# Second layer of an adaptive feed-forward network: the last four blocks in 256-token strips, gates after the fold product, and another order of the low-rank chunks

## The chip, the cores and the metric

The kernel runs on one core of a Trainium2 chip, in float32. Its time is the device time in microseconds of that core; a median of several runs is compared. The engines are TensorE (PE, with its weight loads as PEld), VectorE (DVE), ScalarE (ACT), GpSimd (POOL) and SyncE (SP), which only issues transfers here.[...]

## The reference, cut to what matters

There are 32 x 128 tokens of width 128. Layer 0 (`x = x + L0_ffn(L0_cond(...))`) is left as it is by the change. Layer 1 is this:

```python
def _L1_cond_ref(x, t_emb, W_router, router_bias, s_w1, s_w3, s_w2, r_w1, r_w2):
    for e in range(N_SHARED):                                    # 2 shared experts, width 256
        h = jax.nn.silu(x_flat @ s_w1[e].T) * (x_flat @ s_w3[e].T)
        shared_out = shared_out + h @ s_w2[e].T
    shared_out = shared_out / N_SHARED
    s = jax.nn.sigmoid((router_in @ W_router.T).astype(jnp.float32))
    ...                                                          # the two best of 8 -> gates_full
    for e in range(N_EXPERTS):                                   # 8 routed experts, width 128
        h = jax.nn.gelu(x_flat @ r_w1[e].T, approximate=False)
        routed_out = routed_out + h @ r_w2[e].T * gates_full[:, e:e + 1]
    return (shared_out + routed_out) / (N_SHARED + TOP_K)

def _L1_ffn_ref(x, U1, V1, b1, U2, V2, b2):                      # rank 32, width 512
    P = jnp.einsum('bsd,dr->bsr', x, U1)
    H = jax.nn.gelu(jnp.einsum('bsr,rf->bsf', P, V1) + b1)
    Q = jnp.einsum('bsf,fr->bsr', H, U2)
    return jnp.einsum('bsr,rd->bsd', Q, V2) + b2

x = x + _L1_ffn_ref(_L1_cond_ref(x, cond, ...), U1, V1, b1, U2, V2, b2)
```

## The kernel before, in words

The tokens lie transposed (128 features on the partitions) in eight blocks of 512 tokens, `xall`; four blocks are a set, `sb` 0 and 1. Layer 0 ends at 800 us of the profile. Its feed-forward part is 64 units of 9.89 us, and its last fold products still lie between the first two units of layer 1.

Nothing of layer 1's middle has the full width: the down weights of its experts are multiplied once with `U1` (`fold`, `fold_down`, L249), so that each expert gives 32 rows per token at once. `into` (L848) puts the 32 rows of four blocks side by side on the four quarters of the 128 partitions, one column tile of TensorE for each block, and adds all experts of a set in one PSUM bank, `p_ps`. The rows of layer 1:

- `sh_up`, `sh_down`: four units per set, one for each half of a shared expert. Each up makes, for each block, a gate and an up product (`by_columns`, L238: four column tiles of 32), Silu on ScalarE and a product on VectorE (`glu`, L649 and L650).
- `r_up`, `r_down`: eight units per set, one per expert. For each block POOL broadcasts a row of gates over 128 partitions (`spread`, L644), ScalarE takes Gelu (L883), and VectorE multiplies by the gates (L884) before the fold product.
- `low_in`, `low_up`, `low_down`, `low_out`: the 32 rows are copied to SBUF (L892), multiplied by a chunk of `V1` in row tiles (L901), Gelu in its tanh form on ScalarE (L902), multiplied by a chunk of `U2` (L848 again, `q_ps`); after four chunks the result is copied (L912), multiplied by `V2` (L916), `b2` and x are added on VectorE (L918), and the block goes out (L920), by turns on SP's and ScalarE's queue.

`pipelined` gives the order: the up of a unit is written ahead of the down of the unit before it. The list `units` is: the feed-forward units; the four shared units of set 0 and then of set 1; the eight routed units of set 0; two routed of set 1; low-rank chunks 0 to 2 of set 0; the other six routed of set 1; the last chunk of set 0; the four chunks of set 1. `after` hangs the router's steps for set 1 on these units: its products and transposes (L536, L551), its Sigmoid (L783), the choice of two (`route`), and `gates_to_dram` with `gate_rows` (L565 to L569, L873), which turn the gates into rows by way of DRAM. The framework writes semaphores itself and may move an instruction within its engine's queue where its planner sees an operand come late.

PSUM has eight banks of 512 columns: six go around as `mm` tiles, two as `y` tiles (`p_ps`, `q_ps`).

## Time and profile before

| what | value |
|---|---|
| median of 3 runs | 971.49 us (970.68 to 971.59) |
| the profiled execution | 971.3 us, its span 969.4 us |
| granted TensorE clock | 0.997 |
| TensorE, weight loads | 956.0 us (99%), 446.5 us (46%) |
| VectorE, ScalarE, POOL | 631.9, 343.9, 142.4 us |
| stretch 909.70 to 969.40 | PE 52.41, DVE 32.86, ACT 36.90, POOL 24.27 us |
| products of N=512 (L238, L848, L901) | 592 to 636 ns each, four side by side |
| Gelu with gates before the fold: L883, L884, L644 | 598, 1001, 1185 ns, 64 times each |
| gelu in tanh form, 512 columns (L902, L263), 256 columns (L507) | 696 and 688, 474 ns |
| ACT_TABLE_LOAD | 1283 ns |

The page gives busy time of each engine, then the span in 40 slices with busy tenths. A record's busy time of a product includes its fill, so products that run side by side or overlap are told apart by their starts. A float32 product is two records. In timelines the columns are start, duration, engine, line, operation, out<-in, tile and shape, count, and in brackets the idle time before and what ended it.

### The profile page before, as it was taken

What the parts mean: (1) busy time and instruction counts of PE and PEld (TensorE: products, weight loads), DVE (VectorE), ACT (ScalarE), POOL (GpSimd) and SP (SyncE); (2) the same over time, 40 slices, a digit from 0 to 9 for tenths busy, and PEclk for the clock granted to TensorE, in tenths of its full rate; (3) what the DMA queues carried; (4) which work ended last, traced back from release to release, by engine and by line L of the source; (5) the groups of instructions that cost most, each with busy time, mean ns of one, the idle gap of its engine ahead of it and who ended that gap; (6) DMA issues with size and microseconds to landing.
All of it is one profiled execution on the core that took longest, in us unless ns stands there. A gap on an engine that the chain in (4) does not pass through costs nothing.

```text
span 969.4 us, 15512 instructions
## 1 busy us (share of the span) xinstructions
PE 956.0 (99%) x5966; PEld 446.5 (46%) x5966; DVE 631.9 (65%) x1130; ACT 343.9 (35%) x615; POOL 142.4 (15%) x150
## 2 busy tenths in 40 slices
PE   8999999999999999999999999999999999999997
PEld 3588984444444444444444444444444443333342
DVE  4444574766856776686677786677668555648593
ACT  5355544233322322232231332232223223435764
POOL 0000002100101010110101011010100001019680
PEclk9999999999999999999999999999999999999998
DMA  9845641000000000000000000000000000000002
GB/s 307 250 148 167 213 135 47 2 1 3 1 1 2 1 1 1 1 1 1 1 2 1 1 2 3 1 1 1 1 1 1 1 3 2 1 7 1 1 2 87
DMA packets 19329, 34.04 MB, mean 35 GB/s; under 512 B 1760, under 2 KB 10464, under 8 KB 19232
## 3 DMA queue, kind: packets, MB, share of 16 engines
q1 hardware_dynamic: 18240, 31.50, 10.4%
q10 hardware_dynamic: 1008, 1.46, 0.4%
q8 instruction: 51, 0.84, 0.4%
q14 instruction: 30, 0.25, 0.1%
HBM read 30.59 MB, written 2.36 MB: 34 GB/s over the span
## 4 chain that ended last, share of the span: by engine, by line
PE 84%; DVE 0%; DVEq 0%; issue 0%
PE g L238 26%; PE u L238 26%; PE ya L731 11%; PE yb L731 9%; PE ur L238 6%; PE p_ps L848 2%; PE ul L901 1%; PE ys L273 1%; PE q_ps L848 1%; PE us L262 1%; PE fold_ps L249 0%; PE o_ps L916 0%; PE lg_ps L536 0%; PE l_ps L536 0%; DVE fin L918 0%; PE l_b L551 0%
## 5 line engine op out<-in xcount | busy, mean ns | idle before, releaser
L649 ACT ACTIVATE sf<-g 128x512 f32<-128x512 f32 x256 | 152.7, 597 | 435.1 <-PE g L238 426.8
L650 DVE TENSOR_TENSOR hf<-sf,u 128x512 f32<-128x512 f32 x256 | 175.0, 686 | 182.7 <-PE u L238 181.8
L238 PE MATMUL g<-c0all,wg_t 128*64 128x512 f32 x1024 | 263.5, 593 | 0.0
L238 PE MATMUL u<-cg,wu_t 128*64 128x512 f32 x1024 | 263.1, 592 | 0.0
L644 POOL PARTITION_BROADCAST fg<-fgT x64 | 72.4, 1142 | 655.7 <-DVE cg L692 494.3
L238 PEld LDWEIGHTS u<-cg,wu_t 128*64 128x64 f32 x1024 | 73.6, 137 | 146.2 <-issue 127.6
L238 PEld LDWEIGHTS g<-c0all,wg_t 128*64 128x64 f32 x1024 | 72.9, 137 | 121.3 <-issue 106.8
L731 PE MATMUL ya<-t,wd_t 128*64 128x256 f32 x512 | 121.0, 379 | 0.0
L644 POOL PARTITION_BROADCAST rg<-grows x64 | 67.6, 1185 | 143.8 <-DVE hr L884 75.5
L884 DVE TENSOR_TENSOR hr<-ar,rg 128x512 f32<-128x512 f32 x64 | 61.1, 1001 | 15.5 <-ACT ar L883 15.4
L731 PEld LDWEIGHTS ya<-t,wd_t 128*64 128x64 f32 x512 | 70.1, 137 | 0.0
L507 ACT ACTIVATE h<-u,w 128x256 f32<-128x256 f32 (+3 forms) x136 | 49.6, 434 | 49.5 <-PE u L504 49.4
L731 PE MATMUL yb<-hf,a_sum 128*64 128x256 f32 x512 | 66.1, 379 | 0.0
L731 PE MATMUL ya<-hf,wd_t 128*64 128x256 f32 x256 | 65.7, 379 | 0.0
L731 PE MATMUL ya<-t,a_sum 128*64 128x256 f32 x256 | 65.7, 379 | 0.0
L711 DVE TENSOR_TENSOR hf<-hf 128x512 f32<-128x512 f32 x64 | 63.0, 985 | 2.1
L238 PE MATMUL ur<-xall,rw_t 128*32 128x512 f32 x512 | 58.4, 592 | 0.0
L731 PEld LDWEIGHTS ya<-hf,wd_t 128*64 128x64 f32 x256 | 35.0, 137 | 46.0 <-issue 36.8
L520 PE MATMUL y<-h,w 128*128 128x256 f32 (+3 forms) x272 | 52.6, 338 | 0.5 <-DVE t L523 0.5
L504 PE MATMUL u<-x,w 128*128 128x256 f32 (+3 forms) x272 | 52.2, 337 | 0.0
L883 ACT ACTIVATE ar<-ur 128x512 f32<-128x512 f32 x64 | 37.9, 598 | 27.6 <-PE ur L238 27.0
L504 PEld LDWEIGHTS u<-x,w 128*128 128x128 f32 x272 | 45.3, 190 | 4.4 <-issue 0.7
(211 smaller groups left out, 916.8 us busy)
## 6 DMA issues: line engine op xcount, KB each, us to landing
w<-in_experts SPq DMA_DIRECT2D x36, 514.5 KB
wg_t<-in_w_gate SPq DMA_DIRECT2D x8, 256.0 KB
wu_t<-in_w_up SPq DMA_DIRECT2D x8, 256.0 KB
wd_t<-in_w_down SPq DMA_DIRECT2D x8, 256.0 KB
xall<-in_x SPq DMA_DIRECT2D x7, 256.0 KB
out<-fin SPq DMA_DIRECT2D x4, 256.0 KB
out<-fin ACTq DMA_DIRECT2D x4, 256.0 KB
downs<-in_r_w SPq DMA_DIRECT2D x2, 256.0 KB
```

Of the source, the lines that this page charges most:

```text
L238: nc.tensor.matmul(ps[own, :], lhsT=w[:, own], rhs=x, start=True, stop=True)
L504: nc.tensor.matmul(ps[c][:, :m, :n], lhsT=w1, rhs=x[:, :m, :n], start=True, stop=True)
L507: nc.scalar.activation(h[:, c, :m, :n], ps[c][:, :m, :n], AF.Gelu_apprx_tanh, bias=bias)
L520: nc.tensor.matmul(y[:, :m, :n], lhsT=w2, rhs=h[:, c, :m, :n], start=(c == 0), stop=(c == NC - 1))
L644: nc.gpsimd.partition_broadcast(bc, row)
L649: nc.scalar.activation(s, ps_gate, AF.Silu)
L650: V.tensor_tensor(h, s, ps_up, ALU.mult)
L711: V.tensor_tensor(b12, b12, b11, ALU.subtract)
L731: nc.tensor.matmul(y[half, n], lhsT=w[:, c, :], rhs=h[:, c, :], start=first, stop=(e == EF - 1 and last))
L848: nc.tensor.matmul(y[32 * j : 32 * (j + 1), :], lhsT=w, rhs=h[:, j, :], start=first, stop=last)
L883: nc.scalar.activation(a, ps, AF.Gelu)
L884: V.tensor_tensor(h[:, j, :], a, gate, ALU.mult)
```

## The change

Layer 1 is put into three groups: set 0 as it was (four strips of 512 tokens), blocks 4 and 5 as one group and blocks 6 and 7 as another, with four strips of 256 tokens each. Then:

- All PSUM banks become one tile; `mm_tile` and `y_tile` deal them in a fixed ring, `mm_banks` gives two or four neighbours. The gelu of a low-rank chunk reads two banks (group 0) or four half banks (groups 1 and 2), 1024 columns, in one instruction.
- The routed gates are applied behind the fold product, on the 32 rows of four strips: `r_down` writes a bank of its own for each expert, VectorE multiplies it by gates that were broadcast from DRAM by the transfer itself (`gate_rows`, 12 transfers in place of 8), and adds it to the sum in SBUF.
- Low-rank chunks of the group before are written among the shared units and the first routed unit of the next group (`low_half`).
- In layer 1 TensorE's and ScalarE's instructions are pinned to program order; `table` writes a one-element activation ahead of each change of function.
- For the last group the chunks use fixed banks, two of the four outputs get x by an identity product in PSUM and `b2` on ScalarE, and blocks 6 and 7 go out in halves.

The removed functions are those printed above. The diff, cut:

```diff
@@ -110,11 +110,26 @@
+    NM, NY = 6, 2
+    banks = psum.tile([P, NM + NY, TB], F32, tag="banks", name="banks", bufs=1)
+    taken = {"mm": 0, "y": 0}
     def mm_tile(name):
-        return psum.tile([P, TB], F32, tag="mm", name=name, bufs=6)
+        taken["mm"] += 1
+        return banks[:, (taken["mm"] - 1) % NM, :]
     def y_tile(name):
-        return psum.tile([P, TB], F32, tag="y", name=name, bufs=2)
+        taken["y"] += 1
+        return banks[:, NM + (taken["y"] - 1) % NY, :]
+    def mm_banks(n):
+        at = -(-taken["mm"] // 2) * 2
+        if at % NM + n > NM:
+            at = -(-at // NM) * NM
+        taken["mm"] = at + n
+        return banks[:, at % NM : at % NM + n, :]
...
@@ -235,7 +250,9 @@
         for at in range(0, P, n):
             own = slice(at, at + n)
-            nc.tensor.matmul(ps[own, :], lhsT=w[:, own], rhs=x, start=True, stop=True)
+            mm = nc.tensor.matmul(ps[own, :], lhsT=w[:, own], rhs=x, start=True, stop=True)
+            if n < 64:
+                tc.keep_in_program_order(mm)
...
-        in_dram[kind, sb] = d.rearrange("(g k b) t -> k g (b t)", g=2, k=4)
+        in_dram[kind, sb] = d.rearrange("(e b) t -> e (b t)", e=E1)
...
-        nc.scalar.activation(of_sb(l1, sb), of_sb(l1, sb), AF.Sigmoid)
+        sigmoid = nc.scalar.activation(of_sb(l1, sb), of_sb(l1, sb), AF.Sigmoid)
+        if sb > 0:
+            in_order(sigmoid)
...
+    GROUPS = ((0, 4, TB), (4, 2, TB // 2), (6, 2, TB // 2))
+    low_p, low_q_ps = {}, {}
+    tiny = const([1, 1], "tiny")
+    def table(func):
+        if held.get("table") != func:
+            in_order(nc.scalar.activation(tiny, ones[:1, :1], func))
+            held["table"] = func
+    def into(y, w, strips, first, last):
+        for j, h in enumerate(strips):
+            in_order(nc.tensor.matmul(y[32 * j : 32 * (j + 1)], lhsT=w, rhs=h, start=first, stop=last))
+    def strips_of(h, group):
+        n = GROUPS[group][2]
+        return [h[:, b, at : at + n] for b in range(h.shape[1]) for at in range(0, TB, n)]
+    def sh_up(group, k, of=None, h=None):
+        table(AF.Silu)
+        e, c = divmod(k, 2)
+        if h is None:
+            h = work.tile([P, SB, TB], F32, tag="h", name=f"hs_{group}_{k}", bufs=3)
+        for at, b in enumerate(blocks(group)):
+            if of in (None, at):
+                g, u = mm_tile(f"g1_{b}_{k}"), mm_tile(f"u1_{b}_{k}")
+                by_columns(g, sws_t[0][:, e, c, :], x1T[b], 32)
+                by_columns(u, sws_t[1][:, e, c, :], x1T[b], 32)
+                in_order(glu(g, u, h[:, at, :], f"s1_{b}_{k}"))
+        return h
+    def sh_down(group, k, h):
+        _, n, size = GROUPS[group]
+        if k == 0:
+            held["shared", group] = y_tile(f"p_ps{group}")[:, :size]
+        y = held["shared", group]
+        into(y, fold[:, k, :], strips_of(h[:, :n, :], group), k == 0, k == 3)
+        if k == 3:
+            low_p[group] = work.tile([P, 2, TB], F32, tag="gT", name=f"pT{group}")[:, 0, :size]
+            V.tensor_copy(low_p[group], y)
+    gates_t = [
+        wpool.tile([P, E1, TB], F32, tag=tag, name=f"gates{sb}") for sb, tag in enumerate(("wg", "wu"))
+    ]
+    def gate_of_strips(e, group):
+        if group == 0:
+            return gates_t[0][:, e, :]
+        return gates_t[1].rearrange("p e (g t) -> p e g t", g=2)[:, e, group - 1, :]
+    def gate_rows(sb):
+        rows = in_dram["r", sb]
+        for group in (0,) if sb == 0 else (1, 2):
+            n = GROUPS[group][2]
+            for j in range(SB):
+                at = (max(group, 1) - 1) * SB * n + j * n
+                to = gates_t[sb][32 * j : 32 * (j + 1)]
+                if group > 0:
+                    to = to.rearrange("p e (g t) -> p e g t", g=2)[:, :, group - 1, :]
+                nc.sync.dma_start(out=to, in_=rows[:, at : at + n].partition_broadcast(32))
+    def experts_of(group, i):
+        return (i,) if group == 0 else (2 * i, 2 * i + 1)
+    def r_up(group, i, of=None, h=None):
+        table(AF.Gelu)
+        if h is None:
+            h = work.tile([P, SB, TB], F32, tag="h", name=f"hr_{group}_{i}", bufs=3)
+        pieces = [(e, b) for e in experts_of(group, i) for b in blocks(group)]
+        for at, (e, b) in enumerate(pieces):
+            if of is None or e == experts_of(group, i)[of]:
+                ps = mm_tile(f"ur_{b}_{e}")
+                by_columns(ps, rw1_t[:, e, :], x1T[b], 32)
+                in_order(nc.scalar.activation(h[:, at, :], ps, AF.Gelu))
+        return h
+    def r_down(group, i, h):
+        _, n, size = GROUPS[group]
+        for at, e in enumerate(experts_of(group, i)):
+            y = y_tile(f"py_{group}_{e}")[:, :size]
+            into(y, fold[:, 2 * 2 + e, :], strips_of(h[:, at * n : (at + 1) * n, :], group), True, True)
+            t = work.tile([P, TB], F32, tag="sg", name=f"pg_{group}_{e}", bufs=4)[:, :size]
+            V.tensor_tensor(t, y, gate_of_strips(e, group), ALU.mult)
+            V.tensor_tensor(low_p[group], low_p[group], t, ALU.add)
+    def by_rows(ps, w, t, j, first=True):
+        own = slice(32 * j, 32 * (j + 1))
+        in_order(nc.tensor.matmul(ps, lhsT=par32[own, w], rhs=t[own, :], start=first, stop=True))
+    def low_gelu(h, ps, c):
+        in_order(nc.scalar.activation(h, ps, AF.Gelu_apprx_tanh, bias=col("b1", c)))
+    def low_up(group, c):
+        table(AF.Gelu_apprx_tanh)
+        h = work.tile([P, SB, TB], F32, tag="h", name=f"hl_{group}_{c}", bufs=3)
+        for two in (slice(0, 2), slice(2, 4)):
+            ps = mm_banks(2)
+            for k in range(2):
+                by_rows(ps[:, k, :], v1(c), low_p[group], two.start + k)
+            low_gelu(h[:, two, :], ps, c)
+        return h
+    def low_up_two(group, c, ps):
+        table(AF.Gelu_apprx_tanh)
+        h = work.tile([P, SB, TB], F32, tag="h", name=f"hl_{group}_{c}", bufs=3)
+        h = h.rearrange("p j (c t) -> p c j t", c=2)
+        for k in range(2):
+            for j in range(SB):
+                by_rows(ps[:, j, k * HALF : (k + 1) * HALF], v1(c + k), low_p[group], j)
+        for k in range(2):
+            low_gelu(h[:, k], ps[:, :, k * HALF : (k + 1) * HALF], c + k)
+        return h
+    def low_down(group, c, h, q=None):
+        n = GROUPS[group][2]
+        if c == 0:
+            low_q_ps[group] = (y_tile(f"q_ps{group}") if q is None else q)[:, :n]
+        into(low_q_ps[group], col("u2", c * 32, 32), [h[:, j] for j in range(SB)], c == 0, c == NC - 1)
+    def low_down_two(group, c, h, q=None):
+        for k in range(2):
+            low_down(group, c + k, h[:, k], q)
+    def low_q(group):
+        n = GROUPS[group][2]
+        q = work.tile([P, TB], F32, tag="lgT", name=f"qT{group}", bufs=1)[:, :n]
+        V.tensor_copy(q, low_q_ps[group])
+    def strip(group, j):
+        first, n, size = GROUPS[group]
+        b, half = divmod(j, SB // n)
+        return first + b, slice(half * size, (half + 1) * size)
+    def low_out(group):
...
-    STAGES = {"f": (ffn_up, ffn_down), "s": (sh_up, sh_down), "r": (r_up, r_down), "l": (low_up, low_down)}
-    units = [("f", blk, e) for blk, e in ffn_units]
-    units += [("s", sb, k) for sb in range(NS) for k in range(4)]
-    units += [("r", 0, e) for e in range(E1)]
-    units += [("r", 1, 0), ("r", 1, 1)]
-    units += [("l", 0, c) for c in range(NC - 1)]
-    units += [("r", 1, e) for e in range(2, E1)]
-    units += [("l", 0, NC - 1)]
-    units += [("l", 1, c) for c in range(NC)]
...
+            b, at = strip(group, j)
+            ps = mm_tile(f"o_ps{group}_{j}")[:, : at.stop - at.start]
+            by_rows(ps, AT32["v2"], held["qT", group], j)
+            if at.start == 0:
+                t = work.tile([P, TB], F32, tag="fin", name=f"fin{b}", bufs=4)
+            V.scalar_tensor_tensor(t[:, at], ps, col("b2"), x1T[b][:, at], ALU.add, ALU.add)
+            if at.stop == TB:
+                nc.sync.dma_start(out=out[b], in_=t)
...
+        elif unit == ("s", 0, 2):
+            table(AF.Sigmoid)
             l1_scores(1)
-        if (kind, sb, i) == ("s", 1, 1):
+        elif unit == ("r", 0, 1):
             gates_to_dram("r", 1)
             gate_rows(1)
...
+    STAGES = {"f": (ffn_up, ffn_down), "s": (sh_up, sh_down), "r": (r_up, r_down)}
+    units = [("f", blk, e) for blk, e in ffn_units]
+    units += [("s", 0, k) for k in range(4)] + [("r", 0, e) for e in range(E1)]
+    units += [("s", 1, 0)]
+    h = STAGES["f"][0](*units[0][1:])
+    for unit, after in zip(units, units[1:]):
+        ahead = STAGES[after[0]][0](*after[1:])
+        STAGES[unit[0]][1](*unit[1:], h)
+        in_front_of_l1(unit)
+        h = ahead
+    for group in (1, 2):
+        of = group - 1
+        r = None
+        def low_half(c, next_part, h):
+            if of == 0:
+                l0 = low_up(of, c)
+                sh_down(group, c + 1, h)
+                part = next_part(0, None)
+                l1 = low_up(of, c + 1)
+                low_down(of, c, l0)
+                taken["mm"] += 2
+                next_part(1, part)
+                low_down(of, c + 1, l1)
+            else:
+                l = low_up_two(of, c, mm_banks(SB))
+                sh_down(group, c + 1, h)
+                part = next_part(0, None)
+                low_down_two(of, c, l)
+                next_part(1, part)
+            return part
+        h1 = sh_up(group, 1)
+        sh_down(group, 0, h)
+        h2 = low_half(0, lambda part, t: sh_up(group, 2, part, t), h1)
+        h3 = sh_up(group, 3)
+        sh_down(group, 2, h2)
+        r = low_half(2, lambda part, t: r_up(group, 0, part, t), h3)
+        low_q(of)
+        for i in range(1, E1 // 2):
+            ahead = r_up(group, i)
+            r_down(group, i - 1, r)
+            r = ahead
+            if i == 1:
+                low_out(of)
+        if group == 1:
+            h = sh_up(2, 0)
+        r_down(group, E1 // 2 - 1, r)
+    last = [(c, low_up_two(2, c, banks[:, 2 * c : 2 * c + SB, :])) for c in (0, 2)]
+    for c, h in last:
+        low_down_two(2, c, h, banks[:, 0, :])
+        if c == 0:
+            for j in (2, 3):
+                b, at = strip(2, j)
+                in_order(
+                    nc.tensor.matmul(banks[:, j, :HALF], lhsT=ident, rhs=x1T[b][:, at], start=True, stop=False)
+                )
+    low_q(2)
+    fins = [work.tile([P, TB], F32, tag="fin", name=f"fin{b}", bufs=4) for b in blocks(2)]
+    for j, bank in enumerate((1, 4, 2, 3)):
+        by_rows(banks[:, bank, :HALF], AT32["v2"], held["qT", 2], j, first=j < 2)
+    for j, bank in enumerate((1, 4, 2, 3)):
+        b, at = strip(2, j)
+        t = fins[j // 2][:, at]
+        if j < 2:
+            V.scalar_tensor_tensor(t, banks[:, bank, :HALF], col("b2"), x1T[b][:, at], ALU.add, ALU.add)
+        else:
+            in_order(nc.scalar.activation(t, banks[:, bank, :HALF], AF.Identity, bias=col("b2")))
+    for j in (0, 2, 1, 3):
+        b, at = strip(2, j)
+        queue = nc.scalar if j == 3 else nc.sync
+        queue.dma_start(out=out[b][:, at], in_=fins[j // 2][:, at])
```

## The prediction

> **What bounds the kernel now.** I read the page first: engine shares and the 40 slices.
>
> ```profile
> span 969.4 us, 15512 instructions
> PE 956.0 (99%) x5966; PEld 446.5 (46%) x5966; DVE 631.9 (65%) x1130; ACT 343.9 (35%) x615; POOL 142.4 (15%) x150
> PE   8999999999999999999999999999999999999997
> ACT  5355544233322322232231332232223223435764
> ```
>
> TensorE is busy throughout, so outside L1 (800.5 us on) nothing in this change can save time. The chain that ended last is 84% PE. Busy is no proof of full pace, so next I read TensorE's timeline in L1 and compare starts.
>
> ```profile
> 866.71 3.62 PE L238 MATMUL ur<-xall,rw_t 128*32 128x512 f32 x32
> 870.14 1.04 PE L848 MATMUL p_ps<-hs,fold 128*32 128x512 f32 x8
> 871.00 3.62 PE L238 MATMUL ur<-xall,rw_t 128*32 128x512 f32 x32
> ...
> 908.77 1.04 PE L848 MATMUL p_ps<-hr,fold 128*32 128x512 f32 x8
> 909.74 1.14 PE L901 MATMUL ul<-pT,par 32*128 32x512 f32 x8
> ...
> 957.84 3.51 PE L848 MATMUL q_ps<-hl,par 128*32 128x512 f32 x16
> 962.13 1.14 PE L916 MATMUL o_ps<-qT,par 32*128 32x512 f32 x8 [0.78 <-DVE qT L912]
> ```
>
> Four column-tile products (x8 records, two per fp32 product) start 0.858 us after the four before (870.14 to 871.00); call that a group. A routed unit is five groups, 4.29 us. This pace holds without a gap from 800 to 909.63 (908.77 + 0.86). From there to the end of the last q products 48 groups are left: down of routed expert 1 (1), low-rank chunks 0 to 2 of set 0 (6), six routed units (30), the last chunk of set 0 (2), its output (1), four chunks of set 1 (8). That is 41.2 us, due at 950.8; they end at 961.35. So **10.5 us are lost**: 1.8 between 909.63 and 916.59, the rest after 942.3, where ScalarE and not TensorE sets the pace. The timeline of all engines there:
>
> ```profile
> 909.02 0.60 ACT L883 ACTIVATE ar<-ur 128x512 f32<-128x512 f32 x1 [0.26 <-DVE hr L884]
> 909.63 1.28 ACT L902 ACT_TABLE_LOAD   x1
> 910.93 7.15 ACT L902 ACTIVATE hl<-ul,par 128x512 f32<-128x512 f32 x12
> ...
> 953.15 7.09 ACT L902 ACTIVATE hl<-ul,par 128x512 f32<-128x512 f32 x12 [3.72 <-DVE fin L918]
> ...
> 961.38 0.69 DVE L912 COPY qT<-q_ps 128x512 f32<-128x512 f32 x1 [8.66 <-PE q_ps L848]
> ...
> 963.29 2.72 DVE L918 SCALAR_TENSOR_TENSOR fin<-o_ps,par,xall 128x512 f32<-128x512 f32 x4 [1.21 <-PE o_ps L916]
> ```
>
> The reader is to see twelve gelus without a gap (0.59 us each) and then a serial end: copy, product, four additions, transfers, 961.35 to 969.4 = 8.05 us. **What can be won is inside these 10.5 + 8.05 us.**
>
> **The change, part by part.**
>
> *Arithmetic.* Column counts on TensorE stay. Folds and low-rank products of the last four blocks are twice as many with N=256. No row has N=256 in 32-column tiles; the nearest is L731, N=256 in 64-column tiles, 16 records in 1.73 us, where 1.71 is half of four groups' 0.858: no overhead. The Trainium skill, "TensorEngine Tiling (Array Packing)", section "Instruction Overhead", gives some 60 cycles per matmul; eight records then need an estimated 0.2 us, less than 0.43. I take 0.43 and keep 0.43 to 0.6 for the range.
>
> *Gates behind the fold product.* 64 gatings on VectorE (1.00 us each, L884) and 64 broadcasts on POOL (1.19 us, L644) go. Added: per expert one multiplication and one addition, 0.69 us (0.42 at 256 columns, the L758 to L773 rows): 1.4 us in a unit of 4.29. Both are hidden by TensorE before and after; without that cover the old 4.0 us per unit would still fit. Gate rows now come by 12 broadcasts on SP, 4.2 MB in place of 0.13: at the 380 GB/s of the last transfers 5.5 us per half, 47 us of room for the first (797 to 844) and 50 for the second. SP has nothing else queued there. Zero. The second router transpose is now pinned ahead of routed products, at 848.4; VectorE's route work, done at 849.1 before, has two gated products' operations added and two SwiGLU products fewer: +0.3 us.
>
> *Order up to the second set.* Set 0 does four shared units, then eight routed ones at 4.29, the next shared unit's up in the last: TensorE is there at 839.7 + 8 x 4.29 + 0.5 (transpose and mode changes) = **874.5**. Left are 89.5 groups to the last q product (group 1: 43; the up between: 4; group 2: 38.5; last chunks without output: 4), 76.8 us, so 951.3 with no wait.
>
> *Mode changes.* ul starts 0.11 us after the group before it would end (909.63 to 909.74), and so back. Sixteen such: +1.8.
>
> *Low-rank chunks amid shared experts.* Before, L1 changed the activation table six times; now 17 times, each with a tiny activation (0.1 us beyond overlap, from the 0.20 us of a 32x4 row). **Here a rule speaks against the change.** Row: the last Gelu ends at 909.62, the load runs 909.63 to 910.91, the next gelu starts at 910.93: 1.30 us. The skill, "ScalarE: Activation LUTs", section "What ACT_TABLE_LOAD costs": 1.28 plus a drain of about 1.38, together 2.66 us. I take the row, with 0.1 for the tiny activation: 1.4. A two-bank gelu of 1024 columns: 0.688 (512) + 2 x 0.214 (the step from 256, 0.474) = 1.12, and 1.02 back to back.
> The first half-stage of group 1: the tanh load may start at 877.9; gelus from 879.6 to 881.7; Silu load to 883.1, two silus to 884.1 less overlap, 883.5; tanh load to 884.9; next gelu to 886.0. TensorE needs that gelu's two banks at 883.5 for the second part of the shared up (bank numbers: 775 allocations so far, six in the ring, and the step of two): **2.6 us waiting**. The half with routed products the same way: 3.1. In group 2 each half has two switches (2.8), 2.0 of gelus and 2.0 of silus against 5.8 of TensorE and 3.4 of cover after it: none. With the skill's figure these waits are about 14.7 in place of 5.7. The second r_down pair ahead of the end waits 0.7 on gelu latency and its bank.
>
> Routed end: 874.5 + 85.5 x 0.858 + 1.8 + 5.7 + 0.7 = **956.0**.
>
> *The end.* Fold product to multiplication 0.24, then 0.43 + 0.45: 957.1. Low-rank products and fill 0.85: gelus from 957.95, four: 3 x 1.01 + 1.12: 962.1. First two q products 960.1 to 961.0, two identity products 0.86 + 0.22 of changes, last two q products to 963.0, fill 0.2: 963.2, **1.8 later than now**. Copy 0.43, product 0.73 (half of 0.858, plus the 0.3 of latency in the 1.14 row): 964.4; two additions each on VectorE and ScalarE 0.9: 965.3 (now 966.0). Transfers: now 1.05 MB at 380 GB/s, first packet 0.74 us after the first addition, last packet 967.8, 1.6 to the end. Then 0.52 MB; the third issue on SP, 0.5 apart, sets it: 965.9 + 0.4 + 0.34 + 1.6 = **968.2**. End part: 5.0 in place of 8.05.
>
> **Sum**, on the span: lost time gone -10.5; shorter end -3.0; waits for tables +5.7; mode changes +1.8; r_down +0.7; the last set's serial stretch (956.0 to 963.2 = 7.2 for 3.4 of work) +3.8; transpose and rounding +0.3. Together **-1.2**: 968.2. The profiled execution took 971.3 (1.9 around its span), the median is 971.49, 0.2 above it; the prediction is made on the median: **970.3**.
>
> **Rivals.**
> 1. *The table loads stay hidden.* For: ScalarE is busy 37 of 59.7 us here (stretch 909.7 to 969.4), and TensorE can run six banks ahead. Against: the bank that the shared part needs is that of the gelu behind the second load. Waits 5.7 to about 1: 965.6.
> 2. *Slower: a switch costs more than its row.* One mechanism, in the two halves of group 1, eight switches in a chain. Between 1.30 and 2.66 the waits grow 9.0 us, 6.6 per us of switch; from 1.8 us per switch on (3.1 more than the sum) the change is slower by over 0.2%. At 2.66: 979.3. Against: 1.30 is measured, twice (909.63 and 918.09, hl to ar). For: Silu with tanh in alternation has no row in L1.
> 3. *N=256 products run slower in 32-column tiles.* At 0.50 us +1.7, at 0.60 +4.2: 974.5; slower from 0.56 on. Against: the L731 row.
> 4. *Nothing changes*, because all is hidden: excluded, the 10.5 lost us are not hidden.
>
> **How the numbers follow.** What this kernel's measurement can tell from no change is about 0.2%, 1.9 us. The sum 0.50, own range 968 to 972.5: 0.20 of it below 969.5 and 0.30 within the bound. Rival 1 0.22, rival 2 0.20, rival 3 0.08. Faster 0.42, same 0.30, slower 0.28. The range for 8 in 10 cuts the lower quarter of rival 1 and the upper half of rival 2: 965.0 to 976.5.
>
> **What would show it.** Right: TensorE still at 0.858 per group up to some 874; two waits of 2.5 to 3 us at up products near 884 and 898, released by gelus behind ACT_TABLE_LOAD; group 2 gapless; four 1024-column gelus of 1.1 us, then a last transfer issued near 966. Wrong: loads with idle ScalarE around them (rival 2), fold products of 256 columns over 0.5 us apart (rival 3), no wait in group 1 (rival 1), a wait on gate rows, or a feed-forward unit off its 9.89 us because PSUM banks are now dealt in a fixed ring.

## The result: 0.5% slower

The changed kernel takes **976.62 us** (median; 974.71 to 977.59), the kernel before 971.54 us (970.68 to 972.93) in the same session: a ratio of **1.0048, 95% interval 1.0035 to 1.0061**. The prediction had 970.3 us, 0.1% faster. The profiled execution took 976.8 us, its span 975.0 us, where the sum had 968.2: 6.8 us have to be explained.

The page of the changed kernel, the lines that answer to those shown of before:

```profile
span 975.0 us, 15713 instructions
PE 955.6 (98%) x6138; PEld 444.8 (46%) x6138; DVE 593.3 (61%) x1118; ACT 358.1 (37%) x630; POOL 75.1 (8%) x86
PE   8999999999999999999999999999999999998996
ACT  5445544232322322232232332232223223558674
```

POOL's broadcasts and a good part of VectorE's products are gone as the diff says (142.4 to 75.1 us, 631.9 to 593.3), and nothing comes of it. TensorE's busy time is what it was, yet the span is 5.6 us longer. The view of TensorE's waits names the largest item:

```profile
PE banks L253 <- ACT hl L980: 5.2, 2, 2.8
...
PE banks L890 <- ACT hl L980: 1.4, 1, 1.4
PE banks L972 <- DVE pT L967: 1.3, 1, 1.3
PE banks L279 <- ACT hs L280: 0.9, 1, 0.9
```

Columns: who waits for whom, us in total, times, longest. The first line is the pair of waits that was predicted; it comes to 5.2 us in the trace and 5.6 by starts (5.7 predicted). TensorE's timeline shows what was not:

```profile
883.56 1.07 PE L890 MATMUL banks<-hl,par 128*32 128x512 f32 x8
887.00 3.41 PE L253 MATMUL banks<-xall,sws 128*32 128x512 f32 x16 [2.38 <-ACT hl L980]
890.17 1.31 PE L890 MATMUL banks<-hl,par 128*32 128x512 f32 x8
891.30 3.62 PE L253 MATMUL banks<-xall,sws 128*32 128x512 f32 x32
...
899.70 1.07 PE L890 MATMUL banks<-hl,par 128*32 128x512 f32 x8
903.60 2.95 PE L253 MATMUL banks<-xall,rw_t 128*32 128x512 f32 x16 [2.83 <-ACT hl L980]
906.30 1.78 PE L890 MATMUL banks<-hl,par 128*32 128x512 f32 x8
907.89 3.62 PE L253 MATMUL banks<-xall,rw_t 128*32 128x512 f32 x32
```

From 887.00 to 891.30 lie three groups of four column-tile products (x16 and x8), 2.57 us at 0.858 each; they take 4.30. From 903.60 to 907.89 the same three take 4.29. Nothing is waited for inside either stretch. The windows of the trace give the reason; columns are the stretch, its length, busy time of PE, PEld, DVE, ACT, POOL with counts, then the granted TensorE clock:

```profile
884.50:887.00 2.50, 0.12 (x4) 0.00 (x0) 0.66 (x1) 2.49 (x4) 0.00 (x0) 1.00 0.00 0
887.00:887.50 0.50, 0.50 (x4) 0.16 (x8) 0.00 (x0) 0.50 (x1) 0.00 (x0) 0.79 0.00 0
887.50:890.50 3.00, 3.00 (x20) 0.85 (x16) 0.00 (x0) 2.41 (x4) 0.00 (x0) 0.50 0.00 0
890.50:891.00 0.50, 0.50 (x8) 0.13 (x4) 0.47 (x1) 0.00 (x0) 0.00 (x0) 0.80 0.00 0
891.00:894.00 3.00, 3.00 (x36) 0.91 (x29) 0.88 (x2) 0.60 (x1) 0.00 (x0) 1.00 0.00 0
...
904.00:904.50 0.50, 0.50 (x8) 0.13 (x4) 0.00 (x0) 0.50 (x1) 0.00 (x0) 0.86 0.00 0
904.50:907.50 3.00, 3.00 (x20) 0.85 (x16) 0.00 (x0) 2.60 (x5) 0.00 (x0) 0.50 0.02 5
907.50:908.00 0.50, 0.50 (x8) 0.10 (x4) 0.00 (x0) 0.00 (x0) 0.00 (x0) 0.73 0.00 0
```

**After each wait TensorE runs at half its clock for 3.4 us**: 20 records in 3 us instead of 36. (A window of 0.5 us at 0.79 holds 0.21 us at half clock; so, with the other windows read likewise, the two stretches run from 887.29 to 890.70 and from 904.36 to 907.77.) By the starts of the products that costs 1.73 and 1.72 us, 3.45 us that my sum had no line for. On the page's slices the clock reads 9 everywhere, and over the span 0.995 for 0.997: only windows of half a microsecond show it.

ScalarE in front of the first wait, which is as predicted:

```profile
882.47 1.28 ACT L880 ACT_TABLE_LOAD   x1
883.76 0.20 ACT L880 ACTIVATE tiny<-ones 1x1 f32<-1x1 f32 x1
883.87 0.57 ACT L667 ACTIVATE s<-banks 128x512 f32<-128x512 f32 x1
884.46 1.28 ACT L880 ACT_TABLE_LOAD   x1
885.75 0.20 ACT L880 ACTIVATE tiny<-ones 1x1 f32<-1x1 f32 x1
885.86 2.08 ACT L980 ACTIVATE hl<-banks,par 128x1024 f32<-128x1024 f32 x2
```

A switch costs 1.28 for the load and 0.1 for the one-element activation, 1.40 from the load's start to the start of the next activation that does work (882.47 to 883.87). The first of the last two gelus ends near 886.9, and TensorE starts at 887.00.

The end, in the timelines of TensorE, ScalarE and VectorE:

```profile
960.76 0.64 PE L890 MATMUL banks<-hr,fold 128*32 128x256 f32 x8 [0.15 <-DVE pg L966]
962.73 2.01 PE L972 MATMUL banks<-pT,par 32*128 32x256 f32 x32 [1.33 <-DVE pT L967]
964.00 4.13 ACT L980 ACTIVATE hl<-banks,par 128x1024 f32<-128x1024 f32 x4 [2.92 <-PE banks L972]
969.44 0.42 DVE L1018 COPY qT<-banks 128x256 f32<-128x256 f32 x1 [6.77 <-PE banks L890]
970.65 0.88 DVE L1135 SCALAR_TENSOR_TENSOR fin<-banks,par,xall 128x256 f32<-128x256 f32 x2 [0.79 <-PE banks L972]
```

The part from the last q products to the end of the span is shorter than before, 5.7 us for 8.05. But from the end of the last fold product (961.2) to the first of the four gelus (964.0) it is 2.8 us, 0.9 more than in my sum, and ScalarE is idle meanwhile.

### The profile page after: what moved, and what is told of

Same layout as the page of the kernel before. It is cut to its first block, busy times and chain, and to the rows that moved or that the text cites. A ratio compares the mean times of both kernels' runs of the same rounds, so it can differ in the third digit from the quotient of the medians.

```text
span 975.0 us, 15713 instructions
## 1 busy us (share of the span) xinstructions
PE 955.6 (98%) x6138; PEld 444.8 (46%) x6138; DVE 593.3 (61%) x1118; ACT 358.1 (37%) x630; POOL 75.1 (8%) x86
## 4 chain that ended last, share of the span: by engine, by line
PE 82%; ACT 1%; issue 0%; DVE 0%; ACTq 0%; DVEq 0%
PE banks L253 56%; PE banks L750 20%; PE banks L890 3%; PE banks L290 1%; PE banks L972 1%; ACT hl L980 1%; ACT L880 1%; PE banks L279 0%; PE banks L553 0%; PE banks L266 0%; PE banks L568 0%; DVE pT L967 0%; DVE pg L966 0%; PE banks L1125 0%; ACT hr L957 0%
## 5 line engine op out<-in xcount | busy, mean ns | idle before, releaser
L667 ACT ACTIVATE sf<-banks 128x512 f32<-128x512 f32 x256 | 152.7, 597 | 435.2 <-PE banks L253 421.4
L668 DVE TENSOR_TENSOR hf<-sf,banks 128x512 f32<-128x512 f32 x256 | 174.8, 685 | 183.3 <-PE banks L253 182.4
L253 PE MATMUL banks<-c0all,wg_t 128*64 128x512 f32 x1024 | 263.4, 593 | 0.0
L253 PE MATMUL banks<-cg,wu_t 128*64 128x512 f32 x1024 | 263.1, 592 | 0.0
L253 PEld LDWEIGHTS banks<-cg,wu_t 128*64 128x64 f32 x1024 | 73.4, 137 | 146.3 <-issue 127.1
L253 PEld LDWEIGHTS banks<-c0all,wg_t 128*64 128x64 f32 x1024 | 72.8, 137 | 121.4 <-issue 108.8
L750 PE MATMUL banks<-t,wd_t 128*64 128x256 f32 x512 | 121.0, 379 | 0.0
L750 PE MATMUL banks<-hf,wd_t 128*64 128x256 f32 x512 | 104.2, 379 | 0.0
L750 PEld LDWEIGHTS banks<-t,wd_t 128*64 128x64 f32 x512 | 70.1, 137 | 0.0
L750 PE MATMUL banks<-hf,a_sum 128*64 128x256 f32 x512 | 66.1, 379 | 0.0
```

The lines of the kernel that those rows point to most:

```text
L253: mm = nc.tensor.matmul(ps[own, :], lhsT=w[:, own], rhs=x, start=True, stop=True)
L667: silu = nc.scalar.activation(s, ps_gate, AF.Silu)
L668: V.tensor_tensor(h, s, ps_up, ALU.mult)
L750: nc.tensor.matmul(y[half, n], lhsT=w[:, c, :], rhs=h[:, c, :], start=first, stop=(e == EF - 1 and last))
```

## The experiments

All times are medians beside the kernel before on the same chip (971.23 to 971.80 there); the last column is from the first product of layer 1 to the end of the profiled span (differences of it are taken before rounding). It leaves out how the program starts: layer 0's feed-forward part began between 165.4 and 167.3 us from one profiled execution to another, also among kernels that are the same up to there.

| kernel | median us | ratio to before, 95% interval | L1 to the end, us |
|---|---|---|---|
| before | 971.54 | | 168.9 |
| changed | 976.62 | 1.0048 (1.0035 to 1.0061) | 173.8 |
| x1: no step of two banks | 972.04 | 1.0004 (0.9996 to 1.0012) | 169.5 |
| x2: products in the waits | 973.20 | 1.0016 (1.0008 to 1.0025) | 170.8 |
| x3: two chunks together | 969.26 | 0.9976 (0.9967 to 0.9985) | 166.8 |
| x4: before, with the ring | 972.51 | 1.0011 (1.0005 to 1.0018) | 169.4 |
| x5: before, with the gates | 973.13 | 1.0019 (1.0013 to 1.0026) | 170.7 |
| x6: x3, needless switches | 972.03 | 1.0008 (0.9999 to 1.0016) | 169.5 |
| x7: x3, a gelu for each bank | 969.51 | 0.9979 (0.9973 to 0.9986) | 167.0 |
| x8: x3, folds behind, no load ahead | 973.08 | 1.0017 (1.0010 to 1.0024) | 170.5 |
| x9: one function in a half | 968.93 | 0.9972 (0.9961 to 0.9983) | 165.7 |
| x10: x3, folds behind | 968.98 | 0.9975 (0.9964 to 0.9985) | 166.5 |
| x11: x3, no load ahead | 973.82 | 1.0022 (1.0013 to 1.0031) | 171.0 |
| x12: x5, with loads ahead | 970.78 | 0.9995 (0.9987 to 1.0003) | 168.0 |

**Theory**: the table loads make TensorE wait twice in group 1, and idling that long halves its clock afterwards. **Rivals**: each load costs more than its row, or the ring, the gates or the products of 256 columns are what is slow.

### x1: the wait made shorter

```diff
                 low_down(of, c, l0)
-                taken["mm"] += 2
                 next_part(1, part)
```

> The changed kernel with one line less: the step of two in the ring of PSUM banks is gone, so the second part of the next unit gets banks 4 and 5 (read by the Silu and its product, done at 884.4 and 885.2) in place of 0 and 1 (read by the gelu that ends at 887.0). Theory (two waits of 2.6 and 2.8 us behind the activation tables, each followed by some 3.5 us at half the TensorE clock, which costs 1.7 more): the wait becomes several short ones of about 1.5 us in all per half and the clock stays up; 971.5 us, 5 less than the changed kernel, and no stretch at clock 0.50 before the end. Rival (the waits alone cost, the clock is an accident of that run): 974.5. Rival (the loss is elsewhere, as in N=256 products or gate transfers): 976.5.

Measured 972.04, 4.6 us below the changed kernel. Other banks come due, TensorE's waits fall to 0.58 and 1.06 us, and the windows after them stay at clock 1.00. Waits 3.6 us shorter and 3.45 us of slow clock would be 7.0, and the last column has 4.3; with the other banks the q and up products now also alternate in small portions on TensorE, and where the rest goes was not followed further. The run doesn't separate the two terms; x2 does.

### x2: the same wait, with TensorE busy

```diff
                 low_down(of, c, l0)
+                idle = banks[:, taken["mm"] % NM, :]
                 taken["mm"] += 2
+                for _ in range(3):
+                    in_order(nc.tensor.matmul(idle, lhsT=ident, rhs=x1T[0], start=True, stop=True))
                 next_part(1, part)
```

> The changed kernel with more work: in each of the two waits TensorE makes three full products of N=512 (2.6 us) that nobody reads, in a bank that the ring steps over. They change no dependence of other work; only the array is not idle. Clock theory: no stretch at 0.50 after the waits, 3.2 us less than the changed kernel, 973.4. Rival (the clock does not matter, or falls for another reason): the same 976.6, or up to 0.5 more for the mode changes.

Measured 973.20: **six more products that nobody reads make the kernel 3.4 us faster.** The timeline and a window of this kernel:

```profile
884.03 1.07 PE L890 MATMUL banks<-hl,par 128*32 128x512 f32 x8
885.03 2.84 PE L1090 MATMUL banks<-xall,ident 128*128 128x512 f32 x6
887.80 1.92 PE L253 MATMUL banks<-xall,sws 128*32 128x512 f32 x16
```

```profile
887.80:890.80 3.00, 3.00 (x29) 0.94 (x32) 0.35 (x1) 2.59 (x4) 0.00 (x0) 1.00 0.00 0
```

The wait is still there, now filled: from the q products at 884.03 to the up products at 887.80 is 3.77 us, in the changed kernel 3.44 (883.56 to 887.00). Behind it the clock is 1.00, and the two groups take 1.92. The second wait has the same length in both, 3.90 us. So 3.45 of clock less 0.33 is 3.1, and the last column of the table has 3.0: length and clock are two costs.

### x3: fewer switches, shorter waits

Both chunks of a half are written together ahead of the up products, so that group 1 has one pair of switches in a half in place of two (13 loads in place of 17).

```diff
                 sh_down(group, c + 1, h)
-                part = next_part(0, None)
                 l1 = low_up(of, c + 1)
+                part = next_part(0, None)
                 low_down(of, c, l0)
-                taken["mm"] += 2
                 next_part(1, part)
```

> The changed kernel with the first set's low-rank chunks written two at a time, as the second set's are: both low-rank ups, then both parts of the next unit, so two changes of activation table per half in place of four (13 in layer 1 in place of 17), and no step of two. Theory (table changes make the waits): waits under 1 us per half, clock at full speed, 968 to 969.5 us, 7 to 8 less than the changed kernel and 2 to 3 less than before. Rival (PSUM banks are what is short, so that two chunks with eight banks wait as long): 975 to 977.

Measured 969.26, **faster than both kernels**: 0.24% below before. TensorE:

```profile
879.14 0.64 PE L890 MATMUL banks<-hs,fold 128*32 128x256 f32 x8
879.71 1.85 PE L972 MATMUL banks<-pT,par 32*128 32x512 f32 x8
881.50 1.92 PE L253 MATMUL banks<-xall,sws 128*32 128x512 f32 x16
```

The second chunk's products take 1.79 us from start to start for 0.86 of work: two of the four have to wait until the first gelu gives their banks back (880.44), so they run two by two and not four side by side. That is 0.93 us, and 0.90 in the other half. By starts that is 3.8 us of waits gone, with 3.45 of slow clock 7.2; the last column of the table has 7.1.

### x9: the same order without the loads

Set 0's chunks take Silu (0 and 1) and Gelu (2 and 3) in place of the tanh form, whose function group 1's other activations have anyway. This leaves the tanh form of those chunks out; order, banks and the step of two stay as in the changed kernel.

```diff
-        table(AF.Gelu_apprx_tanh)
+        func = AF.Silu if c < 2 else AF.Gelu
+        if c == 2:
+            table(func)
...
-            low_gelu(h[:, two, :], ps, c)
+            low_gelu(h[:, two, :], ps, c, func)
```

> The changed kernel with its order, banks and the step of two untouched, but the low-rank chunks of the first set take the function of the unit that they stand among (Silu for chunks 0 and 1, Gelu for 2 and 3) in place of gelu in tanh form, so their activations need no change of table: 10 loads in layer 1 in place of 17. The part left out is the tanh form of those chunks' gelu; their size and count stay. Theory (the loads make the two waits, the waits make the clock fall): both waits under 0.7 us, no stretch at 0.50, 967 to 969 us. Rival (order or banks make the waits, as the two banks are those of a gelu that is late anyway): over 974.

Measured 968.93. The first wait in its trace:

```profile
883.33 1.07 PE L890 MATMUL banks<-hl,par 128*32 128x512 f32 x8
884.60 1.92 PE L253 MATMUL banks<-xall,sws 128*32 128x512 f32 x16 [0.20 <-ACT hl L980]
```

The waits shrink to 0.41 and 0.37 us by starts (884.19 to 884.60, 896.50 to 896.87). Loads gone, waits gone: the loads are their cause. It is 8.2 us in the last column: 4.8 of waits and 3.45 of clock.

### x6: two needless switches in each half

In x3, Silu is called for between the gelus of the two chunks and tanh again.

```diff
                 sh_down(group, c + 1, h)
+                table(AF.Silu)
                 l1 = low_up(of, c + 1)
```

> The kernel with the low-rank chunks of group 1 two at a time (969.3), and in each half of group 1 one needless change to Silu and back between the gelus of the first chunk and those of the second: four loads and four one-element activations more, 1.4 us each. No product is added. Theory A (two terms): the two TensorE waits of 0.9 us grow by 2.8 to about 3.7 each, +5.6, and after each the granted clock is half for some 3.5 us, +1.7 each: 969.3 + 5.6 + 3.4 = 978.3 (977 to 979.5). Theory B (the waits alone, no clock): 974.9 (974 to 976). If the loads were hidden: no more than 970.

Measured 972.03, which neither theory had. The price of a switch was right, the cover was not: ScalarE is some 2.9 us later (the second pair of gelus starts at 885.56, 5.06 us behind the first, where the gelus of x3 follow each other without a gap), but TensorE has work until 885.33 and starts at 886.70.

```profile
884.47 1.04 PE L890 MATMUL banks<-hl,par 128*32 128x512 f32 x8
886.70 1.92 PE L253 MATMUL banks<-xall,sws 128*32 128x512 f32 x16 [1.19 <-ACT hl L980]
```

1.37 us in each half, 2.7 together, as measured (+2.8). I had added the 2.8 us of the switches to a wait of 0.9 that is a different one, at the banks of the second chunk, and it didn't grow. What the run is worth is its clock: in the profiled execution an idle time of 1.19 us leaves the two groups behind it at 1.92 us, full pace.

### x7: how much the gelu over several banks gives

Each low-rank gelu of x3 in two halves.

```diff
-        in_order(nc.scalar.activation(h, ps, AF.Gelu_apprx_tanh, bias=col("b1", c)))
+        n = h.shape[1]
+        for k in range(0, n, max(1, n // 2)):
+            part = slice(k, k + max(1, n // 2))
+            in_order(
+                nc.scalar.activation(h[:, part], ps[:, part], AF.Gelu_apprx_tanh, bias=col("b1", c))
+            )
```

> The version with two changes of table per half, with each low-rank gelu split in two of 512 columns. By the rows 1.02 us for 1024 columns becomes 2 x 0.59: 0.15 us more for each of 16. Theory (ScalarE's queue is the chain only in the first set's two halves and at the end): 0.6 us in each of these three, 1.2 to 2 us more than the version it starts from, 970.5 to 971.3. Rival (a bank is given back earlier, which TensorE waits for): 968 to 969.

Measured 969.51, 0.25 above x3, and the two ranges overlap. In the last set the halves take 4.73 us where the whole gelus take 4.13, and TensorE's wait for the first of them falls from 1.44 to 1.13 us, since its banks come back earlier: both of what was expected, and the two nearly cancel. The other sets were not followed.

### x8, x11 and x10: what the one-element activations do

x8 makes two edits to x3 at once, and so can't tell them apart: the fold product of each half behind the first low-rank chunk, and the one-element activations dropped.

```diff
-        if held.get("table") != func:
-            in_order(nc.scalar.activation(tiny, ones[:1, :1], func))
-            held["table"] = func
+        held["table"] = func
...
-                sh_down(group, c + 1, h)
+                sh_down(group, c, h_before)
```

> The version with two changes of table per half, and two more edits: the fold product that stood ahead of each half is written behind its first low-rank chunk, where TensorE otherwise waits for the first gelu's banks (0.43 us of work in each of two waits of 0.7 to 0.9), and the one-element activations go. 0.8 to 1.3 us less than the version it starts from: 968.0 to 968.5, below both kernels. If those waits are covered by something else: 969.3.

Measured 973.08. x10 makes the first edit alone (the fold products), x11 the second.

> The kernel with the low-rank chunks of group 1 two at a time (969.3), without the one-element activations ahead of each change of function; nothing else differs. Theory A: a table load whose instruction waits for an operand of TensorE's stands behind that operand, so at most of the 13 changes the load is late by what it could have run ahead; in the last set that is 1.3 us of later gelus and a TensorE wait of about 2.7 us, with half the clock for some 3 us after it. Together 2.5 to 4.5 us: 972 to 973.8. Theory B: loads go ahead by themselves as before the change (909.63, with no wait shown), and leaving out 13 activations of 0.2 us gains a little: 968.5 to 969.3.

> The kernel with the low-rank chunks of group 1 two at a time, and the fold product of each half written behind the first low-rank chunk instead of ahead of it; the one-element activations stay. It does one of the two edits of the run in which both were made (973.1 against 969.3). Theory A: the loss of 3.8 us came from the one-element activations that were dropped there, as the load in the last set then stood behind the products (956.57) and TensorE's idle 2.7 us halved its clock; the moved fold products cover part of the two waits of 0.9 us. Then 968.0 to 969.3. Theory B: the moved fold products cost it, because the down part's operand and its bank come later: 972 to 973.5.

Measured 973.82 and 968.98: **the one-element activations are worth 4.6 us**, the moved fold products nothing that can be told from none. ScalarE and TensorE in the last set of x11, and a window behind:

```profile
957.95 1.28 ACT L978 ACT_TABLE_LOAD   x1 [4.42 <-PE banks L970]
959.25 4.13 ACT L978 ACTIVATE hl<-banks,par 128x1024 f32<-128x1024 f32 x4
```

```profile
956.69 2.01 PE L970 MATMUL banks<-pT,par 32*128 32x256 f32 x32 [1.33 <-DVE pT L965]
961.42 1.47 PE L888 MATMUL banks<-hl,par 128*32 128x256 f32 x16 [2.71 <-ACT hl L978]
962.82 2.08 PE L1122 MATMUL banks<-xall,ident 128*128 128x256 f32 x4
```

```profile
962.00:963.00 1.00, 1.00 (x13) 0.19 (x3) 0.00 (x0) 1.00 (x2) 0.00 (x0) 0.50 0.00 0
```

The load stands behind the products that its gelu reads (4.42 idle, released by them), though ScalarE had been free all that time. TensorE's wait in the end grows by 1.3, to 2.71 us idle, and the clock halves again: from the first q products to the output product it is 5.34 us in place of 3.75. In the second half of group 1 another 1.3 goes the same way. In x3 a one-element activation, which waits for no product, calls for the table, and the load is ahead of all this (951.40, its gelus at 955.83). Not every load needs that: in the first half of group 1 of x11 it follows the last Silu at once (878.34).

### x4: the ring of banks

The kernel before, with PSUM as one tile and its banks dealt in the fixed ring of six and two; nothing else.

```diff
+    banks = psum.tile([P, NM + NY, TB], F32, tag="banks", name="banks", bufs=1)
     def mm_tile(name):
-        return psum.tile([P, TB], F32, tag="mm", name=name, bufs=6)
+        taken["mm"] += 1
+        return banks[:, (taken["mm"] - 1) % NM, :]
```

> The kernel before, with one part of the change alone: all PSUM banks are one tile and are dealt in a fixed ring of six and two. Theory (part of the loss lies in layer 0, where a product waits 0.9 us for a gelu of an older bank at 147 us): feed-forward units start at 166.6 in place of 165.9 and the time is 0.5 to 0.8 us more than before. Rival (that shift is jitter of the first transfers): no difference, 971.5.

Measured 972.51, +0.7. The last column has 0.5 of it in layer 1: TensorE waits twice in the last low-rank chunks, for a gelu and for an output addition, where before has no such wait.

```profile
949.69 0.69 PE L907 MATMUL banks<-pT,par 32*128 32x512 f32 x1 [0.93 <-ACT hl L908]
952.51 1.78 PE L907 MATMUL banks<-pT,par 32*128 32x512 f32 x4 [0.83 <-DVE fin L924]
```

In layer 0, at 147.2 us, TensorE waits 0.91 us for an activation (the line with L279 among the waits above), in every kernel with the ring and not in before. But before idles 0.84 us at 143.3, where these kernels do not, so that this wait is not shown to cost anything. The changed kernel began layer 1 at 801.17 where before began at 800.46; among the profiled executions with the ring this ranges from 799.95 to 801.98, among the three without it from 800.11 to 800.46. So its 0.7 us are not assigned to the ring.

### x5 and x12: the gates

x5 is the kernel before, with the gates behind the fold product and fetched by broadcasting transfers.

```diff
-            a = work.tile([P, TB], F32, tag="sg", name=f"ar_{sb}_{e}_{j}", bufs=4)
-            nc.scalar.activation(a, ps, AF.Gelu)
-            V.tensor_tensor(h[:, j, :], a, gate, ALU.mult)
+            nc.scalar.activation(h[:, j, :], ps, AF.Gelu)
...
+        y = y_tile(f"py_{sb}_{e}")
+        into(y, fold[:, 2 * 2 + e, :], h, True, True)
+        V.tensor_tensor(t, y, gates_t[sb][:, e, :], ALU.mult)
+        V.tensor_tensor(held["p", sb], held["p", sb], t, ALU.add)
```

> The kernel before, with another part of the change alone: the gates are applied behind the fold product, with gate rows broadcast by the transfer (4.2 MB), and the sum of the experts is kept in SBUF; units, order and PSUM tiles stay. My step (both forms are hidden behind TensorE, the transfers have 47 us of room): 0 to 1 us less than before, 970.5 to 971.5, since the 1.8 us lost at 909.6 to 916.6 hung in part on the slow gatings. Rival (transfers or the y banks, one of which q_ps holds, make fold products wait): 973 or more.

Measured 973.13: a loss where I expected none. No transfer and no VectorE operation is late before 909 us. What moved is a table load:

```profile
910.59 1.28 ACT L903 ACT_TABLE_LOAD   x1 [1.33 <-PE ul L902]
911.89 7.09 ACT L903 ACTIVATE hl<-ul,par 128x512 f32<-128x512 f32 x12
```

In the kernel before, the same load follows the last Gelu at once (909.63). Here it stands behind the low-rank products, and all twelve gelus with it; at 944.60 the same once more. x12 adds one-element activations ahead of these two switches, and pins them and the gelus of both kinds to program order on ScalarE (the cut shows the first).

```diff
         at = AT32["v1"].start + c * P
+        if (sb, c) in ((0, 0), (0, NC - 1)):
+            tc.keep_in_program_order(nc.scalar.activation(tiny, ones[:1, :1], AF.Gelu_apprx_tanh))
```

> The kernel before with the gates behind the fold product (973.1, against 971.2 for the kernel before beside it), and with a one-element activation in the tanh form written ahead of low-rank chunk 0 and of chunk 3 of set 0; order and arithmetic are the same otherwise. Theory A: what that kernel lost was the place of two table loads, which stood 1.3 us behind the products that their gelus read (910.59 and 944.60, in place of right behind the last Gelu); with the loads ahead the end comes 1.4 us earlier, and the gates themselves cost nothing: 971.0 to 971.9. Theory B: the loss is in the sum, which needs a multiplication and an addition behind the last fold product, or in the bank that the products of one expert take: 972.7 to 973.5.

Measured 970.78, with the loads ahead again:

```profile
909.48 1.28 ACT L902 ACT_TABLE_LOAD   x1
910.77 0.20 ACT L902 ACTIVATE tiny<-ones 1x1 f32<-1x1 f32 x1
910.88 7.04 ACT L908 ACTIVATE hl<-ul,par 128x512 f32<-128x512 f32 x12
```

So the gates cost nothing in themselves, 0.9995 of before; the loss was the place of the loads. That pinning alone would not have moved them was not tested. Why the compiled load goes ahead of the operand's wait in before and behind it in x5 was not found out; with the gates moved, the gelus' output buffers were last written by ScalarE and no longer by VectorE, but that this is the reason is only a guess.

## Why the prediction was wrong

The sum's terms beside what the trace of the changed kernel shows, on the span:

| term | predicted | measured | difference |
|---|---|---|---|
| start of layer 1 (cause not shown) | 0 | 0.7 | +0.7 |
| waits for tables in group 1 | 5.7 | 2.58 + 3.04 | -0.1 |
| half clock behind these waits | no term | 1.73 + 1.72 | **+3.45** |
| mode changes, eight visits | 16 x 0.11 = 1.8 | 8 x 0.33 = 2.6 | +0.85 |
| waits in the second `r_down` pair | 0.7 | 0.40 + 0.36 | +0.1 |
| from the last fold product to the end | 956.0 to 968.2 = 12.2 | 961.2 to 975.0 = 13.8 | +1.6 |

Together 6.6 of the 6.8; 0.2 is not assigned.

- **The step that failed** is "waits for tables +5.7". Their place, cause, releaser and length were right (884.4 to 887.0 and 900.6 to 903.6, a gelu behind the second load), but each was priced as its length alone, and the work behind it at 0.858 us per group. Idle TensorE had a second price, 1.7 us each time. x2 shows it as a cost by itself. Without it the changed kernel would stand at 976.62 - 3.45 = 973.2, inside the bound of 0.2%, though still above the sum's own range (968 to 972.5) by the smaller terms of the table; with it, it is slower beyond doubt.
- A rule bears on this, and my sum left it out. The Trainium skill, "TensorE: Matmul & The Clock Gate", section "Why this matters for your kernels", warns of idle gaps above some 3 us, at the cost of half the clock. My two waits were 2.6 and 3.1 us in my own sum: one at the edge, to be taken into the range at least. Here 2.38 us without a product was enough, so the measurement goes further than the rule.
- **Mode changes**: the row I took (909.63 to 909.74) is the way in. The way out costs 0.21 (879.13 to 880.20 is 1.07 for 0.86 of work), so a visit is 0.33 and not 0.22.
- **The end**: gelus 4.13 for 4.15, right. The sum of gated parts was 1.5 us behind the last fold product, not 1.1, since the multiplications and additions of four experts queue on VectorE. The first gelu came 1.27 us after its products began, not 0.85: its banks hold two chunks, and the product that releases it is the last of the second. The span ended 3.5 us after the last addition, not 2.9.
- **The start**: "a feed-forward unit off its 9.89 us because PSUM banks are now dealt in a fixed ring" was named as a way to be wrong. The units kept their pace. x4 puts the ring at 0.7 us, 0.5 of it in the last chunks, for which the changed kernel deals its banks otherwise; its own 0.7 us ahead of layer 1 stay open.
- **Right**: 0.858 us per group up to the fold product that ends at 875.15 (874.5 predicted, plus the 0.7 of the later start), group 2 without a gap, products of 256 columns at half the time of 512 (rival 3 is out: 0.43 from start to start, as at 911.33), the gates at no cost (x12), the shorter part behind the last q products.
- **Rival 2** ended on the right side for the wrong reason. A switch costs 1.40 us with the one-element activation; the drain of 1.38, which the Trainium skill, "ScalarE: Activation LUTs", section "What ACT_TABLE_LOAD costs", adds, doesn't appear between activations here (882.47 to 883.87 above). Rival 1 (loads hidden) is what x9 makes of the kernel by taking loads away, and x3 in part.

## What to carry to other kernels

A wait on TensorE has two prices: its length, and half the clock for 3.4 us behind it once it is long enough (1.7 us lost each time here); look at windows of half a microsecond, since slices and averages hide it. Before switching a table back and forth in a tuned stage, write the work of one function together, and let an activation with no late operand call for the table, so that its load runs while ScalarE is free. A cost found by moving one part alone (x5) may belong to a neighbour that the move displaced.

## What was not expected of the hardware

- The half clock came after idle times of 2.38, 2.71 (x8, x11) and 2.83 us, and not after 0.91, 1.06, 1.19, 1.33 and 1.44 us. Between 1.44 and 2.38 no trace has a case. It set in 0.3 to 0.8 us after TensorE had started again, and in x8 just before.
- The half clock seems to come in fixed steps of time. Both stretches above last 3.41 us, and they begin 17.07 us apart, which is five times 3.41; the one of x11 (961.96 to 965.36) is as long. So the length of a wait may not decide alone, but also where it falls in such a step. Of the 21 executions of x8 one had a mean clock of 1.000, and it is the fastest (971.80, median 973.08): one stretch would have made it 0.998. Two of 11 of x3 (970.45 and 970.50) and two of 13 of x6 (973.09 and 973.38) had 0.997, with no other at so low a clock, and were 1.1 to 1.4 us above the median, so the waits of these kernels, 1.44 us at most, may not be harmless in every execution. None of these five left a trace, and no run moved a wait within a step: this stays open.
- A table load can wait for the operand of the activation that needs it (1.33 us in x5, 4.42 in x11), with ScalarE idle.
